# One gathered chunk in every fourth quad replaced by 128 single-row loads from ScalarE's queue

## The chip, the cores and the metric

The kernel runs on one core of a Trainium2 chip. A core has five engines that run their own instruction streams and meet only through semaphores: TensorE (PE, with its weight loads shown apart as PEld), VectorE (DVE), ScalarE (ACT), GpSimd (POOL) and SyncE (SP), and 16 DMA engines that move data between HBM and the on-chip memories. The metric is device time in microseconds (us) of one execution; lower is better. A profiled execution gives a page of summaries and a trace that can be queried.

## The reference

A layer of a graph network with attention: 12,500 nodes with 128 values, 200,000 edges sorted by destination, four heads of 32 values.

```
h = maximum(layernorm(x), 0)
hn = (h @ W_node.T).reshape(N, 4, 32);  e = (edge_attr @ W_edge.T).reshape(E, 4, 32)
att = sum(concat([hn[src], hn[dst], e], -1) * a, -1)
att = where(att > 0, att, 0.2 * att)
m = maximum(segment_max(att, dst), 0);  ex = exp(att - m[dst])
denom = segment_sum(ex, dst) + (E - deg)[:, None] * exp(-m)
out = x + segment_sum((ex / denom[dst])[:, :, None] * hn[src], dst)
```

The costly part for the memory system is `hn[src]`: one row of a node table for each of the 200,000 edges, in random order.

## The kernel before

A first stage computes, for every node, a row of 137 floats (548 bytes) and writes it to a DRAM tensor `table`: the four heads with a one behind each, a count, and the source's part of the attention logit.

Then the edges are worked off in order. A *group* is 511 edges and one slot that carries a running sum from the group before, so 512 slots: four *chunks* of 128. Four groups are a *quad*; there are 392 groups and 98 quads. A super-stage of mostly four quads (the first two and the last six are shorter) shares one softmax pass.

The source rows of a chunk are fetched by one indirect DMA on GpSimd's queue (line 141): 128 row numbers, one in each partition, give 128 rows of `table` in `ga`, a ring of `QUADS = 8` quads. There are 1494 such gathers from `table`, and 72 early ones that read `x` itself while the table is not yet there.

For a quad, `all_logits` (line 817) does the attention logits of its four groups and `sums` (line 745) weighs and sums its four groups, a few quads later. Both are generators, and `together` (line 150) alternates their steps: a step of `sums` for one group, then a step of `all_logits` for one group of a later quad. The order of all instructions is written out by hand in this way (`tc.manual_schedule()`), and each engine executes its own instructions in that order. `all_logits` starts with `flush` (line 829): `add_sources`, line 580 on VectorE, which adds the sources' logits out of `ga` and so needs the whole quad gathered.

A group of sums runs like this. VectorE scales the rows in `ga` by the softmax weights (line 766) and builds a 0/1 matrix `hot` (line 779); TensorE multiplies chunks 1 to 3 (line 784). Then `complete_group` (line 704) of the group before closes the chain that runs through all groups: VectorE forms the carried sum from the last accumulator (line 709), ScalarE copies its count (line 713), TensorE adds chunk 0 (line 714), and ScalarE copies the accumulator out to `pt` (line 715). Line 709 of the next group waits for that copy. At the end of a quad `divide` (line 790) forms the result rows on VectorE, which go out one group at a time.

SyncE issues every other load and store of this stage, in the same order: for each group a window of input rows `xw`, one of results `out` and one of the side table `pw` (line 504); for each quad the edges' features `ea` (line 302) and the destinations `db` (line 307); for each super-stage `dr` (line 532). The row numbers of the windows are loaded into registers by `windows` (line 488, the load itself line 490). ScalarE issues a few loads at the start and four in `checked` (line 861). The transfers of SyncE and ScalarE together take eight semaphores in turn, in the order of the program: a transfer waits, at its issue, until the one eight places before it has landed.

Of the kernel before, what the change touches and what calls it, by code (L numbers as in the profile page):

```python
# [8 lines left out]
F32 = mybir.dt.float32  # L9
BF16 = mybir.dt.bfloat16  # L10
I32 = mybir.dt.int32
AF = mybir.ActivationFunctionType
OP = mybir.AluOpType
AX = mybir.AxisListType

P = 128
# [8 lines left out]
R_CNT, R_SRC, ROW = H * HW, H * HW + 1, H * HW + 5  # L25

J = 4
GE = J * P
NE = GE - 1
WIN = 96  # L30
SPAN = 80
QG = 4
# [4 lines left out]
AT_ONCE = 4  # L37
RAW, MORE = 4, 2
QUADS = 8
SETS = max(NODE_T, QG * J)  # L40
PAD = 1 << 20


def blocks(total, step):
    return [(i, min(step, total - i)) for i in range(0, total, step)]
# [3 lines left out]
def kernel(  # L49
# [35 lines left out]
    nc = tc.nc  # L85
# [8 lines left out]
    table = dram.tile([NP, ROW], F32, name="table")  # L94
# [27 lines left out]
    quads = blocks(G, QG)  # L122
    nq = len(quads)
# [4 lines left out]

    ga_all = consts.tile([P, QUADS, QG, J, ROW], F32, name="ga")
    GA, GATHERED = {}, set()  # L130

    def gather(q, rows, width, lo, hi):

        g0, m = quads[q]
        ga = GA[q] = ga_all[:, q % QUADS]
        for i in range(lo, hi):
            n = -(-min(E - (g0 + i) * NE + 1, GE) // P)
            if n < J:
                nc.vector.memset(ga[:, i, n:, :], 0.0)
            for j in range(n):  # L140
                nc.gpsimd.indirect_dma_start(  # L141
                    out=ga[:, i, j, 0:width], out_offset=None, in_=rows,
                    in_offset=bass.IndirectOffsetOnAxis(ap=srci[:, g0 + i, j:j + 1], axis=0))

    def held_gather(q, i, rows, width):

        nc.vector.memset(ga_all[0:1, q % QUADS, i, 0, 0:1], 0.0)
        gather(q, rows, width, i, i + 1)
# [8 lines left out]
    with tc.manual_schedule():  # L157
# [6 lines left out]
        for _ in range(AT_ONCE):  # L164
            q, i = early.pop(0)
# [12 lines left out]
        with tc.tile_pool(name="prep", bufs=1) as prep, tc.tile_pool(  # L178
            name="prep_ps", bufs=1, space=bass.MemoryType.PSUM
# [21 lines left out]
        def statistics(pool, rows, T):  # L201


            assert nc.vector.BN_STATS_DIM == 6
            stats = pool.tile([P, SETS, 6], F32, name="stats")
            for t in range(T):
# [15 lines left out]
            nc.vector.scalar_tensor_tensor(shift[:, :T], both[:, :T, 0], -0.5, rstd[:, :T],  # L222
# [81 lines left out]
        def fetch_targets(q):  # L304
            g0, m = quads[q]
            db = DB[q] = load.tile([SPAN, QG, GE], I32, name="db", bufs=2)
            nc.sync.dma_start(db[:, :m, :], dst.rearrange("(g e) -> g e", e=GE)[g0:g0 + m]
                              .unsqueeze(0).to_broadcast([SPAN, m, GE]))

        with tc.tile_pool(name="node", bufs=2) as node, tc.tile_pool(  # L310
            name="node_ps", bufs=2, space=bass.MemoryType.PSUM
        ) as node_ps, tc.tile_pool(name="index", bufs=1) as index, tc.tile_pool(
            name="index_ps", bufs=1, space=bass.MemoryType.PSUM
# [112 lines left out]
            for b, (t0, T) in enumerate(sets):  # L426
# [4 lines left out]
                row = node.tile([P, NODE_T, ROW], F32, name="row")  # L431
# [35 lines left out]
    with tc.tile_pool(name="work", bufs=2) as work, \  # L467
# [17 lines left out]

        U8 = mybir.dt.uint8

        def windows(of, size, g, n):

            return nc.values_load_multi_w_load_instructions(  # L490
                of[0:1, g:g + n], engines=[mybir.EngineType.SP], min_val=0, max_val=(N - 1) * size,
                skip_runtime_bounds_check_because="a destination's row, and that is a node")[1]

        as_bytes = lambda d: d.bitcast(U8)
        rows_at = lambda d, at, size: as_bytes(d.rearrange("n c -> (n c)"))[
            bass.ds(at, SPAN * size)].rearrange("(n c) -> n c", c=size)

        due = {"weights": [], "inputs": [], "results": []}

        def issue(*kinds, all_of=False):  # L500

            for kind in kinds:
                for _ in range(len(due[kind]) if all_of else min(1, len(due[kind]))):
                    nc.sync.dma_start(*due[kind].pop(0))
# [16 lines left out]
        def fetch(q):  # L521
            if q not in EA:
                fetch_features(q)
            fetch_windows(q)
            if q not in GATHERED:
                GATHERED.add(q)
                gather(q, table, ROW, raws(q), quads[q][1])

        def fetch_rows(s):
            g0, m = groups(s)  # L530
            dr = DR[s] = turned.tile([SBG * H, NE + 2], I32, name="dr", bufs=2)
            nc.sync.dma_start(dr[0:H * m, :],
                              dst_rows[g0:g0 + m, :].unsqueeze(0).to_broadcast([H, m, NE + 2]))

        def open_logits(q):
            if q == supers[of_quad[q]][0]:
                fetch_rows(of_quad[q])
            if q + 2 < nq:
                fetch(q + 2)
            AT[q] = work.tile([SPAN, QG, GE], BF16, name="at")  # L540
            LG[q] = ps.tile([P, QG, J, PIECES, H], F32, name="lg")

        def logits(q, i):

            g0, m = quads[q]
            if i >= m:
                return
            ea, db, at, lg = EA[q], DB[q], AT[q], LG[q]
            sw = PW[q][:, i, :]
            nc.vector.tensor_tensor(  # L550
                at[:, i, :], node_ps[0:SPAN, g0 + i:g0 + i + 1].to_broadcast([SPAN, GE]),
                db[:, i, :],
                op=OP.is_equal)
            for w in range(2):
                for j in (2 * w, 2 * w + 1):
                    nc.tensor.matmul(lg[:, i, j].rearrange("p k h -> p (k h)"),  # L556
                                     at[:, i, j * P:(j + 1) * P], sw,
                                     start=i + j == 0, stop=False, skip_group_check=True)
                nc.tensor.matmul(lg[:, i, 2 * w:2 * w + 2, 0, :], ea[:, i, w, :], wblk,  # L559
                                 start=False, stop=True, skip_group_check=True)  # L560
# [129 lines left out]

        begun = []
        state = {}

# [8 lines left out]
        def complete_group(q, i, ga, hot, pt, acc, fc):  # L704
            g0, m = quads[q]
            g = g0 + i
            if g:
                before = state["before"]
                nc.vector.tensor_tensor(  # L709
                    ga[0:1, i, 0, 0:H * HW].rearrange("p (h w) -> p h w", w=HW),  # L710
                    before[WIN:WIN + 1, 0:H * HW].rearrange("p (h w) -> p h w", w=HW),
                    fc.unsqueeze(2).to_broadcast([1, H, HW]), op=OP.mult)
                nc.scalar.copy(ga[0:1, i, 0, R_CNT:R_CNT + 1], before[WIN:WIN + 1, R_CNT:R_CNT + 1])  # L713
            nc.tensor.matmul(acc, hot[:, i, 0, :], ga[:, i, 0, :], start=False, stop=True)  # L714
            nc.scalar.copy(pt[:, i, :], acc)  # L715
            state["before"] = acc

            parts = {nq - 1: (2, 3), nq - 2: (2,), nq - 3: (2,)}.get(q, ())
            if i + 1 in parts or i == m - 1:
                lo = max([k for k in parts if k <= i], default=0)  # L720
                den = work.tile([SPAN, QG, H], F32, name="den")
                nc.scalar.activation(den[:, lo:i + 1, :], pt[0:SPAN, lo:i + 1, R_SRC:R_SRC + H],
                                     AF.Exp, scale=-1.0)
                state["division"] = q, pt, den, lo, i + 1
# [92 lines left out]
        def all_logits(q):  # L817
            flush()
            open_logits(q)
            for i in range(QG):  # L820
                logits(q, i)
                issue("weights")
                if i == QG - 1 and q + 2 < nq:
                    issue("weights", all_of=True)
                    fetch_targets(q + 2)
                yield
            state["logits"] = q

        def flush():

            if "logits" in state:
                add_sources(state.pop("logits"))
# [46 lines left out]
        with tc.manual_schedule():  # L879
# [5 lines left out]

            held = [(q, i) for q in range(raw, min(QUADS, nq)) for i in range(raws(q), quads[q][1])]
            GATHERED.update(range(raw, QUADS))

# [247 lines left out]
```

## Time and profile before

| | us |
|---|---|
| median of three runs (2013.32 to 2015.12) | 2014.33 |
| the profiled execution | 2018.52 |
| its span, first to last instruction | 2016.7 |
| GpSimd busy | 1510.6 |
| TensorE busy | 1369.1 |
| VectorE busy | 1323.2 |
| ScalarE busy | 406.3 |

"Busy" counts an engine's own instructions and, for GpSimd, the making of the descriptors for the gathers; instructions by which the other engines issue a DMA are not counted as busy, though the issuing engine cannot go on to its next instruction before they are done. A group line of the page gives the line, the engine, what is written and read, the count, the busy time and the mean of one, and then the engine's idle time just before and what ended it.

### The profile page before, as it was taken

Reading aid. Unit: us, or ns where it says so; the run is one execution under the profiler, and the core shown is the slowest. Engines: PE = TensorE matmul, PEld = TensorE weight load, DVE = VectorE, ACT = ScalarE, POOL = GpSimd, SP = SyncE. Lnnn points to the kernel's source line nnn. Section 1 sums busy time; section 2 is a strip of 40 time slices with the busy share of each in tenths; the row PEclk is TensorE's granted clock in tenths of the full one; section 3 lists DMA queues with packets and bytes.
Section 4 is the critical chain, followed back from the end, with each engine's and each line's share of the span. In section 5 each row is a group of like instructions: output and inputs, shape, how many; then the busy total and the mean of one; then the engine's idle time right before and its main releaser. Section 6 shows DMA issues by size and latency. Waiting matters only on the chain. (4 is left out here: it accounts for less than half of the span.)

```text
span 2016.7 us, 27090 instructions
## 1 busy us (share of the span) xinstructions
PE 1369.1 (68%) x7317; PEld 1243.8 (62%) x7317; DVE 1323.2 (66%) x3261; ACT 406.3 (20%) x1531; POOL 1510.6 (75%) x1609
## 2 busy tenths in 40 slices
PE   6577888766575757666757666666566666777776
PEld 5567788755565746555656566566565565766665
DVE  6676788666574766655656657556566475668776
ACT  6664122111111111111111111111111111112112
POOL 7777777777777777777777777777777777777774
PEclk8777555555555555555555555555555555555556
DMA  7654756544546455455545454545454545454531
GB/s 251 204 145 118 183 162 178 137 129 130 142 122 156 121 146 138 130 131 136 138 130 147 119 146 123 147 120 147 121 145 120 147 122 144 126 146 125 139 96 36
DMA packets 194091, 279.50 MB, mean 139 GB/s; under 512 B 79849, under 2 KB 143337, under 8 KB 186098
## 3 DMA queue, kind: packets, MB, share of 16 engines
q1 hardware_dynamic: 142128, 165.55, 30.0%
q0 software_dynamic: 50112, 109.61, 21.7%
q10 hardware_dynamic: 1698, 2.58, 0.4%
q8 instruction: 61, 1.00, 0.2%
q14 instruction: 92, 0.75, 0.1%
HBM read 254.25 MB, written 23.30 MB: 138 GB/s over the span
## 5 line engine op out<-in xcount | busy, mean ns | idle before, releaser
L141 POOL DMA_INDIRECT ga<-table,srci x1494 | 1422.9, 952 | 457.7 <-issue 384.0
L784 PE MATMUL acc<-ga,hot 128*97 128x137 f32 x2352 | 645.3, 446 | 54.1 <-ACT ga L759 25.4
L784 PEld LDWEIGHTS acc<-ga,hot 128*97 128x97 f32 x2352 | 516.8, 278 | 70.1 <-ACT ga L759 31.4
L556 PEld LDWEIGHTS <-at 80*128 80x128 bf16 x1568 | 211.0, 163 | 521.7 <-DVE at L550 504.4
L556 PE MATMUL lg<-pw,at 80*128 80x12 bf16 x1568 | 169.1, 181 | 445.8 <-DVE at L550 445.1
L559 PE MATMUL lg<-wblk,ea 128*128 128x8 f32 x1568 | 405.0, 356 | 0.0
L559 PEld LDWEIGHTS lg<-wblk,ea 128*128 128x128 f32 x1568 | 377.4, 306 | 0.0
L580 DVE TENSOR_TENSOR U<-st,ga 128x64 f32<-128x64 f32 x98 | 26.2, 268 | 436.1 <-DMA ga<-table,srci 428.8
L550 DVE TENSOR_TENSOR at<-const_ps,db 80x512 bf16<-80x512 f32 x392 | 267.3, 682 | 6.1
L766 DVE TENSOR_TENSOR ga<-ga,ex_ps 128x528 f32<-128x528 f32 x392 | 268.5, 685 | 0.6 <-issue 0.3
L714 PE MATMUL acc<-ga,hot 128*97 128x137 f32 x784 | 257.4, 431 | 2.8 <-ACT ga L713 2.7
L715 ACT COPY pt<-acc 97x137 f32<-97x137 f32 x392 | 107.4, 274 | 717.5 <-PE acc L714 715.1
L714 PEld LDWEIGHTS acc<-ga,hot 128*97 128x97 f32 x784 | 198.3, 282 | 4.9 <-ACT ga L713 4.6
L709 DVE TENSOR_TENSOR ga<-acc,facs 1x132 f32<-1x132 f32 x391 | 115.8, 296 | 121.8 <-ACT pt L715 111.9
L779 DVE TENSOR_TENSOR hot<-const_ps,slot 128x320 f32<-128x320 f32 x384 | 183.5, 478 | 0.0
L713 ACT COPY ga<-acc 1x1 f32<-1x1 f32 x391 | 59.9, 153 | 459.7 <-DVE ga L709 453.1
L141 POOL DMA_INDIRECT ga<-in_x_dram,srci x72 | 68.8, 955 | 23.1 <-issue 18.6
L807 DVE TENSOR_TENSOR res<-pt,const_ps 80x512 f32<-80x512 f32 (+2 forms) x102 | 67.5, 662 | 3.8 <-DVE const_ps L803 0.3
L811 DVE TENSOR_TENSOR res<-res,xw 80x512 f32<-80x512 f32 (+2 forms) x99 | 67.4, 681 | 3.4
L618 ACT ACTIVATE low<-t_ps 64x511 f32<-64x511 f32 (+2 forms) x28 | 16.5, 589 | 190.5 <-PE t_ps L616 190.5
L398 PE MATMUL row_ps<-wcat,hT 128*128 128x137 f32 x198 | 40.8, 358 | 20.7 <-DVE tgt L404 10.7
L568 DVE TENSOR_REDUCE st<-lg 128x64 f32<-128x192 f32 x98 | 35.0, 357 | 25.5 <-PE lg L559 24.6
(137 smaller groups left out, 1012.8 us busy)
## 6 DMA issues: line engine op xcount, KB each, us to landing
db<-in_dst_dram SPq DMA_DIRECT2D x98, 640.0 KB
ea<-in_edge_t_dram SPq DMA_DIRECT2D x98, 512.0 KB
ga<-table,srci POOLq DMA_INDIRECT x1494
xw<-in_x_dram SPq DMA_DIRECT2D x392, 40.0 KB
out_dram<-res SPq DMA_DIRECT2D x392, 40.0 KB
pw<-side SPq DMA_DIRECT2D x392, 1.9 KB
table<-row SPq DMA_DIRECT2D x9, 616.5 KB
xt<-in_x_dram SPq DMA_DIRECT2D x9, 576.0 KB
```

The lines of the kernel that those rows point to most:

```text
L141: nc.gpsimd.indirect_dma_start(out=ga[:, i, j, 0:width], out_offset=None, in_=rows, in_offset=bass.IndirectOffsetOnAxis(ap=srci[:, g0 + i, ...
L550: nc.vector.tensor_tensor(at[:, i, :], node_ps[0:SPAN, g0 + i:g0 + i + 1].to_broadcast([SPAN, GE]), db[:, i, :], op=OP.is_equal)
L556: nc.tensor.matmul(lg[:, i, j].rearrange("p k h -> p (k h)"), at[:, i, j * P:(j + 1) * P], sw, start=i + j == 0, stop=False, skip_group_ch ...
L559: nc.tensor.matmul(lg[:, i, 2 * w:2 * w + 2, 0, :], ea[:, i, w, :], wblk, start=False, stop=True, skip_group_check=True)
L709: nc.vector.tensor_tensor(ga[0:1, i, 0, 0:H * HW].rearrange("p (h w) -> p h w", w=HW), before[WIN:WIN + 1, 0:H * HW].rearrange("p (h w) -> ...
L714: nc.tensor.matmul(acc, hot[:, i, 0, :], ga[:, i, 0, :], start=False, stop=True)
L715: nc.scalar.copy(pt[:, i, :], acc)
L766: nc.vector.tensor_tensor(val, val, weight.unsqueeze(3).to_broadcast([P, J, H, HW]), op=OP.mult)
L779: nc.vector.tensor_tensor(hot[:, i, :, 0:SPAN], lane_ps.unsqueeze(1).to_broadcast([P, J, SPAN]), slot[:, g, :].unsqueeze(2).to_broadcast([ ...
L784: nc.tensor.matmul(acc, hot[:, i, j, :], ga[:, i, j, :], start=j == 1, stop=False)
L807: nc.vector.tensor_tensor(res[:, :n, :].rearrange("p g (h d) -> p g h d", d=HD), val[:, :, :, 0:HD], share_ps[0:R, :n, :].unsqueeze(3).to_ ...
L811: add.tensor_tensor(res[:, :n, :], res[:, :n, :], xw, op=OP.add)
```

## The change

In quads 12, 16, 20, ..., 96 (22 quads) the last chunk of the last group is no longer gathered. Its 128 rows are loaded by 128 DMAs of one row each from ScalarE's queue into a tile `by_row`, which ScalarE copies to its place in `ga` when the logits of that quad begin. Every `complete_group` issues eight of the rows, four after the copy of line 713 and four after the copy of line 715, so that 16 groups load one chunk; the loading runs about four quads ahead of the use. Eight row numbers at a time are loaded into ScalarE's registers. For each such chunk SyncE loads its 128 source numbers (`of`) and VectorE turns them into byte offsets (`at_row`). After 352 groups there is nothing left to load.

```diff
+AHEAD, EVERY, STEP = 12, 4, 4
...
+    whole = lambda g: E - g * NE + 1 >= GE
+    by_row = [q for q in range(AHEAD, nq, EVERY) if quads[q][1] == QG and whole(quads[q][0] + QG - 1)]
+    is_by_row = lambda q, i, j: q in by_row and (i, j) == (QG - 1, J - 1)
...
             for j in range(n):
+                if is_by_row(q, i, j):
+                    continue
                 nc.gpsimd.indirect_dma_start(
...
-        def windows(of, size, g, n):
+        def windows(of, size, g, n, engine=mybir.EngineType.SP):
...
-                of[0:1, g:g + n], engines=[mybir.EngineType.SP], min_val=0, max_val=(N - 1) * size,
+                of[0:1, g:g + n], engines=[engine], min_val=0, max_val=(N - 1) * size,
...
-        rows_at = lambda d, at, size: as_bytes(d.rearrange("n c -> (n c)"))[
-            bass.ds(at, SPAN * size)].rearrange("(n c) -> n c", c=size)
+        rows_at = lambda d, at, size, n=SPAN: as_bytes(d.rearrange("n c -> (n c)"))[
+            bass.ds(at, n * size)].rearrange("(n c) -> n c", c=size)
...
+        def loaded_by_row():
+            def sources_of(q):
+                g = quads[q][0] + QG - 1
+                of = work.tile([1, P], I32, name="of")
+                nc.sync.dma_start(of, src.rearrange("(o e) -> o e", o=1)[:, (g + 1) * GE - P:(g + 1) * GE])
+                return of
+            of = sources_of(by_row[0]) if by_row else None
+            yield
+            for k, q in enumerate(by_row):
+                at_row = work.tile([1, P], I32, name="at_row")
+                nc.vector.tensor_scalar(at_row, of, float(4 * ROW), None, op0=OP.mult)
+                tile_q = work.tile([P, ROW], F32, name="by_row")
+                for p0 in range(0, P, 2 * STEP):
+                    if p0 == P // 2 and k + 1 < len(by_row):
+                        of = sources_of(by_row[k + 1])
+                    at = windows(at_row, 4 * ROW, p0, 2 * STEP, mybir.EngineType.Activation)
+                    for p in range(2 * STEP):
+                        nc.scalar.dma_start(as_bytes(tile_q[p0 + p:p0 + p + 1, :]),
+                                            rows_at(table, at[p], 4 * ROW, 1))
+                        if p0 + p == P - 1:
+                            ROW_TILES[q] = tile_q
+                        if p % STEP == STEP - 1:
+                            yield
...
                 nc.scalar.copy(ga[0:1, i, 0, R_CNT:R_CNT + 1], before[WIN:WIN + 1, R_CNT:R_CNT + 1])
+            next(row_steps, None)
             nc.tensor.matmul(acc, hot[:, i, 0, :], ga[:, i, 0, :], start=False, stop=True)
             nc.scalar.copy(pt[:, i, :], acc)
             state["before"] = acc
+            next(row_steps, None)
...
             open_logits(q)
+            if q in by_row:
+                nc.scalar.copy(GA[q][:, QG - 1, J - 1, :], ROW_TILES.pop(q))
```

More of the change, by code (lines that the diff above doesn't have):

```diff
@@ L486 @@
         U8 = mybir.dt.uint8
-        def windows(of, size, g, n):
+        def windows(of, size, g, n, engine=mybir.EngineType.SP):
             return nc.values_load_multi_w_load_instructions(
-                of[0:1, g:g + n], engines=[mybir.EngineType.SP], min_val=0, max_val=(N - 1) * size,
-                skip_runtime_bounds_check_because="a destination's row, and that is a node")[1]
+                of[0:1, g:g + n], engines=[engine], min_val=0, max_val=(N - 1) * size,
+                skip_runtime_bounds_check_because="a node's row")[1]
         as_bytes = lambda d: d.bitcast(U8)
-        rows_at = lambda d, at, size: as_bytes(d.rearrange("n c -> (n c)"))[
-            bass.ds(at, SPAN * size)].rearrange("(n c) -> n c", c=size)
+        rows_at = lambda d, at, size, n=SPAN: as_bytes(d.rearrange("n c -> (n c)"))[
+            bass.ds(at, n * size)].rearrange("(n c) -> n c", c=size)
         due = {"weights": [], "inputs": [], "results": []}
@@ L689, in softmax @@
             yield
+        ROW_TILES = {}
+        def loaded_by_row():
[21 more added lines that the diff above has]
+                            yield
+        row_steps = loaded_by_row()
+        next(row_steps)
         begun = []
```

## The prediction

> **What bounds the kernel now.** I read the page's share of each engine first, then its costliest groups, the waits, and then stretches of 16 groups.
>
> ```profile
> span 2016.7 us, 27090 instructions
> PE 1369.1 (68%) x7317; PEld 1243.8 (62%) x7317; DVE 1323.2 (66%) x3261; ACT 406.3 (20%) x1531; POOL 1510.6 (75%) x1609
> ...
> L141 POOL DMA_INDIRECT ga<-table,srci x1494 | 1422.9, 952 | 457.7 <-issue 384.0
> ...
> L580 DVE TENSOR_TENSOR U<-st,ga 128x64 f32<-128x64 f32 x98 | 26.2, 268 | 436.1 <-DMA ga<-table,srci 428.8
> ```
>
> 75% looks like slack, but each gather costs GpSimd 0.952 us and about 0.3 us to get to the next one. The waits of GpSimd show that this 0.3 us is no waiting for anybody: 1320 times, never longer.
>
> ```profile
> POOL ga L141 <- issue: 402.6, 1320, 0.3
> POOL ga L141 <- PE acc L784: 31.7, 104, 0.3
> POOL ga L141 <- DMA ga<-table,srci: 24.1, 79, 0.3
> ```
>
> By the trace, the gathers' start times advance 80 to 81 us per 64 gathers from the first (3 us) to the last (1973 us): 1.255 us each, with no gap. GpSimd is the bound from end to end, and VectorE waits 428.8 us for it at line 580. The pace of the others without that bound can be read too. In the columns below (busy and instruction count of PE, PEld, DVE, ACT, POOL, then clock, DMA share, GB/s) each stretch is 16 groups, from one copy at line 715 to the sixteenth after it.
>
> ```profile
> 243.00:300.00 57.00, 51.10 (x272) 47.61 (x272) 47.37 (x110) 11.61 (x50) 43.08 (x46) 0.50 0.61 164
> 300.00:358.00 58.00, 51.58 (x275) 47.92 (x274) 49.04 (x113) 11.63 (x50) 43.90 (x46) 0.50 0.62 164
> 1078.00:1158.00 80.00, 51.25 (x275) 46.89 (x274) 48.79 (x113) 11.63 (x50) 60.65 (x64) 0.52 0.53 134
> ```
>
> Early, with gathers in hand, 16 groups take 57 to 58 us; later, paced by 64 gathers, 80 us. So the consumers have some 22 us of slack per 16 groups.
>
> **What is removed.** 22 of the 1566 gathers. They lie on the path: 22 x 1.255 = 27.6 us, if nothing else becomes the bound: 2018.5 - 27.6 = 1990.9 in the profiled execution's terms. With 63 gathers instead of 64, GpSimd's pace becomes 79 us per 16 groups; the span ends by it if the consumers keep to about 76 (below).
>
> **What is added, on ScalarE.** For 352 groups ScalarE gets eight row loads, one register load, and once per 16 groups a copy of 128x137. Its own queue in the trace:
>
> ```profile
> 541.22 0.27 ACT L715 COPY pt<-acc 97x137 f32<-97x137 f32 x1 [2.13 <-PE acc L714]
> 541.23 0.34 ACTq L861 DMA_DIRECT2D rows<-in_dst_rows_dram  x1
> 541.61 0.22 ACT L737 CAST hot<-is_last 128x16 f32<-128x16 bf16 x1
> ```
>
> Two things are seen here: a DMA issue holds up the next instruction (the cast starts 0.38 us after it), and it runs beside the copy ahead of it (it starts 0.01 us after the copy). So the copies of line 715 disappear behind row loads, and everything else adds up.
>
> *One row load.* A load of one row at an address from a register is not in the trace. The nearest are SyncE's windows at such addresses: 0.34 to 0.37 us, and the next starts 0.45 us after the last (median of 628 pairs; 0.416 the least).
>
> ```profile
> 1418.14 0.34 SPq L504 DMA_DIRECT2D out_dram<-res  x1
> 1418.59 0.36 SPq L504 DMA_DIRECT2D pw<-side  x1
> 1419.05 0.36 SPq L504 DMA_DIRECT2D xw<-in_x_dram  x1
> ```
>
> Fewer rows are a little cheaper: ScalarE's load of eight partitions (line 861, at 703 us) took 0.30 us against 0.33 for 128. I take 0.42: 0.32 and the 0.10 between. Lower end 0.40. The upper end is `ends_i` at line 317, the only load into one partition: 0.71 us, among neighbours at the start that took 0.36 to 0.62; `dr` (line 532) takes 0.63. With the 0.10 that is 0.73 to 0.81; I keep 0.73 as a rival's price, since 0.71 stood right behind a load of 512 pieces. 128 x 0.42 = 53.8 us per 16 groups.
>
> *The register load.*
>
> ```profile
> L490 SPq TENSOR_LOAD <-base_side x98: 295/305/507, 96.3 to 1913.7; - x98
> ```
>
> To the next instruction 0.36 us, at the 90th percentile 0.54; that is for four numbers, here eight. 16 x 0.36 = 5.8 (up to 8.7).
>
> *ScalarE's own work.* 11.63 us per 16 groups (the row above), less 16 copies of line 715 that are now covered (16 x 0.274 = 4.4), more four stretches of semaphore waits ahead of line 759 (0.27 each at 541.64 to 541.92) and the new copy (about 0.3, as line 759): 8.6 us. In a softmax pass it waits for lines 658, 677 and 682: (50.4 + 45.6 + 21.2) / 28 = 4.2 us with nothing to issue in between; its wait for line 616 shrinks when it comes late, that for line 625 is filled by a group of rows.
>
> Sum without waits for transfers: 53.8 + 5.8 + 8.6 + 4.2 = 72.4 us per 16 groups (66 to 81 with the ends above). That is already 14 us over the unpaced 58 and near the 76.
>
> **The waits for landing.** Each of ScalarE's row loads waits until the transfer eight places before it in the order of the program has landed, SyncE's included (the changed order of instructions shows such a wait at every row). Per group 8 rows and 3 to 5 of SyncE's go over eight semaphores, so a row comes about 2.7 us (5.5 x 0.42 and a register load) after its predecessor was issued. Landing times from the trace's records after 450 us: `pw` 2.0 median (2.6 mean), `xw` 2.5 (3.2), `out` 1.9 (2.4), `db` 5.0 (5.2), `ea` 4.9 (5.2). I take 2.0 for a row. Evenly spread, 186 transfers of 2.35 us mean over eight semaphores need 55 us, less than 72. But ScalarE is in order: behind `db` and `ea` it stands about 5.2 - 2.7 = 2.5 us, and `pt`, line 713 and with them the chain of groups stand with it. The two go out 2.5 us apart (1403.92 and 1406.44 us), so I count one stand per quad, 4 x 2.5 = 10 us. From both sides: 0 (all small ones at 2 us and ScalarE late enough for the big ones) and 28 (rows at 3.4 us, the upper quartile of `pw`; then every second predecessor is late).
>
> By the Trainium skill, DMA: Bandwidth & Descriptors, section Anatomy of one DMA, a small transfer costs a fixed time of about 2.0 us, most of it the receipt of the write, whatever its size. The `pw` median agrees; by that rule rows never hold one another and only `db` and `ea` are left. The same page, section Why a DMA increments its semaphore by 16 and not by 1, has a one-partition transfer run on a single DMA engine, the lowest-numbered, so that all rows would queue on one engine; here `ends_i` shows 2 landing marks where a 128-partition load shows 16, which agrees, and it speaks for the upper end.
>
> **Other engines.** The 22 `of` loads on SyncE (0.35 us each) and the 22 `at_row` on VectorE (about 0.3) lie in slack of both: per 16 groups SyncE waits some 27 us for line 811 alone (657.6 us over 98 quads). Without that cover they cost 22 x 0.65 = 14 us. SyncE's own transfers now wait for rows of the same group, but are fetched one or two quads ahead.
>
> **The sum.** 72.4 + 10 = 82.4 us per 16 groups, against GpSimd's 79. ScalarE becomes the bound, and the early stretches at 57 and 58, where the consumers now catch up with GpSimd, are lost as well. The copy of group 16 stands at 243 us before; then 21 stretches of 82.4 = 1730 us to group 352; the last 40 groups, without rows and with gathers in hand, at 57.5 per 16 with the denser softmax passes and the tail, about 150 (163.6 before, paced). 243 + 1730 + 150 = 2123, and 1.8 around the span: 2125 against 2018.5, or 2121 beside the median of 2014.3 (4.2 lower). No change would be at 77.3 per 16 groups ((2016.7 - 393) / 21), GpSimd's full gain at 76.0 ((1989.1 - 393) / 21).
>
> **The rivals.**
> *ScalarE has room, GpSimd stays the bound (faster).* If ScalarE reaches the big transfers' successors late enough and the sum stays at 72.4, it is under 76.0 and the whole gain comes: 1990.9, beside the median 1987. For it: the sum itself, and the even-spread 55 us. Against: a stand of only 1 us per quad uses up the rest. It decides at 0.9 us per quad. 22%.
> *Near the edge:* 77.1 to 77.5 per 16 groups, within 0.2% (about what can be told from no change here): 2014. 4%.
> *Rows land late.* At 3.4 us per row each of five rows in eight stands 0.7 us: 72.4 + 28 = 100 per 16 groups, 243 + 2100 + 150 = 2493. For it: one partition, and the tail of `pw` (4.6 us at the 90th percentile). Against: 2.0 median. 12%.
> *A one-row issue is dear.* 128 x 0.73 = 93.4 in place of 53.8, landings then covered: 112 per 16 groups, 243 + 2352 + 150 = 2745. For it `ends_i` and `dr`, against it the eight-partition load. 10%.
> *The forecast*, 78 to 90 per 16 groups: 2029 to 2281. 52%.
>
> **How the numbers follow.** Faster 22%, same 4%, slower 74%. Time 2121. The range has to take in the faster case and cuts the two dear ones: 1984 to 2340; the forecast's own is 2029 to 2281.
>
> **What would show it.** Right: GpSimd's row with real waits (longer than 0.3 us, for TensorE or ScalarE to free the ring), line 580 no longer waiting for gathers, ScalarE's queue full of issues 0.42 us apart, ScalarE waiting for `db` and `ea`, line 709 waiting for line 715; 16 groups in 82 us before 2050 and below 65 after. Wrong: gathers still 1.255 us apart to the end, the last at about 1945 us, and line 580 still waiting for them.

## The result, and the profile after

| us | before | after |
|---|---|---|
| median | 2014.12 (runs beside it) | 2256.6 (4 runs, 2254.28 to 2269.23) |
| ratio, 95% interval | | 1.1216 (1.1175 to 1.1258) |
| the profiled span | 2016.7 | 2252.4 |
| start of the last gather | 1973 | 2139 |

The changed kernel is 12% slower. The direction and the cause were as forecast, the size was not: 5% had been forecast. Below, a *stand* is the time for which an engine, ready to issue a transfer, waits because the transfer eight places before it has not landed yet. Lines 704, 709, 713, 715 and 580 of before are 741, 746, 750, 753 and 586 in the changed kernel; the row loads are line 720, their register loads line 496, the gathers line 147.

The page after, its shares and the groups that answer to those shown of before:

```profile
span 2252.4 us, 33202 instructions
PE 1418.9 (63%) x7317; PEld 1251.9 (56%) x7317; DVE 1325.5 (59%) x3283; ACT 420.9 (19%) x1553; POOL 1481.8 (66%) x1587
...
L147 POOL DMA_INDIRECT ga<-table,srci x1472 | 1393.9, 947 | 651.5 <-issue 402.0
...
L746 DVE TENSOR_TENSOR ga<-acc,facs 1x132 f32<-1x132 f32 x391 | 115.9, 296 | 634.5 <-ACT pt L753 626.0
...
L753 ACT COPY pt<-acc 97x137 f32<-97x137 f32 x392 | 107.4, 274 | 823.8 <-DMA by_row<-table 607.8
```

ScalarE shows 19% busy and is the bound, since the issuing of DMAs is not counted and waiting for a landing is not either. What gives it away is the idle time ahead of its copies: 823.8 us ahead of line 753. The waits of the changed kernel say the same (total, times, longest):

```profile
DVE ga L746 <- ACT pt L753: 626.0, 252, 5.8
ACT pt L753 <- DMA by_row<-table: 607.8, 281, 4.4
...
POOL ga L147 <- PE acc L752: 222.4, 97, 17.6
```

VectorE's carried sum, a link of the chain of groups, waits 626.0 us for ScalarE's copy. GpSimd, which before never waited longer than 0.3 us for TensorE, now waits up to 17.6 us for the ring to come free. The wait of VectorE for gathers ahead of the sources' logits (428.8 us before) is no longer in the list.

The same stretches of 16 groups as before, in the changed kernel (columns as in the prediction: length, then PE, PEld, DVE, ACT, POOL, clock, DMA share, GB/s):

```profile
153.00:273.00 120.00, 78.37 (x434) 69.46 (x435) 64.29 (x149) 28.57 (x89) 70.92 (x75) 0.56 0.48 117
273.00:359.00 86.00, 52.83 (x266) 46.43 (x265) 47.89 (x111) 12.56 (x52) 58.40 (x63) 0.50 0.49 122
1016.00:1103.00 87.00, 51.98 (x265) 45.48 (x263) 49.05 (x113) 12.04 (x50) 57.83 (x62) 0.50 0.49 122
2101.00:2166.00 65.00, 50.76 (x270) 46.25 (x268) 55.93 (x132) 14.33 (x57) 29.38 (x32) 0.53 0.49 121
```

16 groups take 86 to 87 us from group 16 on, early and late alike, and 65 once no rows are left (group 352, at 2101 us). GpSimd needs 63 x 1.255 = 79 of the 87 us, so it is no longer the bound.

The 129 us between the forecast's span (2123) and 2252.4 are made up as follows: the first 16 groups took 120 us in place of 92, so that group 16 comes at 273 and not at 243 (30); 21 stretches of (2101 - 273) / 21 = 87.05 in place of 82.4 (98); the tail took 151 in place of 150 (1).

**ScalarE's 87 us, term by term.** The rows and their register loads in the trace:

```profile
L720 ACTq DMA_DIRECT2D by_row<-table x2816: 227/234/492, 150.7 to 2099.8; - x188
...
L496 ACTq TENSOR_LOAD <-at_row x352: 709/769/990, 149.8 to 2096.2; - x176
L496 SPq TENSOR_LOAD <-base_side x98: 295/307/578, 97.8 to 2156.5; - x98
```

A row load takes 0.234 us (median), and two follow each other 0.333 us apart when nothing holds them. The register load of eight numbers takes 0.77 us; the queue turns to the first row behind it, by moving its address, 0.84 us after the load began (median), and this first row takes 0.468, 0.234 more than the others. Rows: 128 x 0.333 + 16 x 0.234 = 46.4; register loads: 16 x 0.84 = 13.4.

The stands are read from the records: ahead of each row its address is moved, and what lies between that move and the row above the usual 0.07 us is the stand. There are two kinds, and one place of the changed kernel's queues shows each. First ScalarE's queue, then SyncE's, over the same time:

```profile
1239.72 1.47 ACTq L720 DMA_DIRECT2D by_row<-table  x4
1241.23 0.27 ACT L753 COPY pt<-acc 97x137 f32<-97x137 f32 x1 [2.31 <-DMA by_row<-table]
1243.57 1.23 ACTq L720 DMA_DIRECT2D by_row<-table  x4
1244.84 0.22 ACT L776 CAST hot<-is_last 128x16 f32<-128x16 bf16 x1 [3.34 <-DMA by_row<-table]
```

```profile
1238.76 0.32 SPq L313 DMA_DIRECT2D db<-in_dst_dram  x1
1239.54 0.32 SPq L510 DMA_DIRECT2D xw<-in_x_dram  x1
1239.96 0.41 SPq L510 DMA_DIRECT2D out_dram<-res  x1
1240.72 0.36 SPq L308 DMA_DIRECT2D ea<-in_edge_t_dram  x1
```

The fifth row of the group shares its semaphore with `db`. ScalarE is ready for it at 1241.31, 2.55 us after `db` went out, and it goes at 1243.57, 4.81 after: a stand of 2.26 us, the kind that was forecast at 2.5. The other kind, 10 us earlier:

```profile
1231.37 0.28 ACT L753 COPY pt<-acc 97x137 f32<-97x137 f32 x1 [2.06 <-DMA by_row<-table]
1233.11 1.46 ACTq L720 DMA_DIRECT2D by_row<-table  x3
```

```profile
1231.31 0.34 SPq L510 DMA_DIRECT2D out_dram<-res  x1
1231.76 0.36 SPq L510 DMA_DIRECT2D pw<-side  x1
1232.22 0.36 SPq L510 DMA_DIRECT2D xw<-in_x_dram  x1
```

Here the predecessor of the row at 1233.11 is the store `out` of 1231.31, which lands in 1.8 us. But SyncE issued it only 0.14 us before ScalarE was ready for the row, since it had waited for the result rows from VectorE; so ScalarE stands for nearly all of the landing.

Summed from group 16 to 352, per 16 groups: behind `db` 10.1 (83 stands of 2.56 us), behind `out` 5.2 (68 of 1.59), `pw` 2.3, `xw` 1.6, behind other rows 0.55, behind `ea` 0.4: 20.1 us. Of the 68 stands behind `out`, 61 began less than 1 us after the store was issued (median 0.14), where over all rows with such a predecessor the median is 2.78. So 46.4 + 13.4 + 20.1 = 79.9 of the 87.05 us. The other 7 are a remainder: ScalarE's own work and its waits in the softmax passes, as far as the rows do not cover them.

### The profile page after: what moved, and what is told of

It is laid out like the page before. It is cut to its first block, busy times and chain, and to the rows that moved or that the text cites. A ratio compares the mean times of both kernels' runs of the same rounds, so it can differ in the third digit from the quotient of the medians.

```text
span 2252.4 us, 33202 instructions
## 1 busy us (share of the span) xinstructions
PE 1418.9 (63%) x7317; PEld 1251.9 (56%) x7317; DVE 1325.5 (59%) x3283; ACT 420.9 (19%) x1553; POOL 1481.8 (66%) x1587
## 5 line engine op out<-in xcount | busy, mean ns | idle before, releaser
L147 POOL DMA_INDIRECT ga<-table,srci x1472 | 1393.9, 947 | 651.5 <-issue 402.0
L823 PE MATMUL acc<-ga,hot 128*97 128x137 f32 x2352 | 647.2, 447 | 388.5 <-ACT ga L798 359.7
L823 PEld LDWEIGHTS acc<-ga,hot 128*97 128x97 f32 x2352 | 517.9, 278 | 409.2 <-ACT ga L798 371.3
L746 DVE TENSOR_TENSOR ga<-acc,facs 1x132 f32<-1x132 f32 x391 | 115.9, 296 | 634.5 <-ACT pt L753 626.0
L752 PE MATMUL acc<-ga,hot 128*97 128x137 f32 x784 | 274.8, 453 | 95.8 <-ACT ga L750 95.4
L562 PEld LDWEIGHTS <-at 80*128 80x128 bf16 x1568 | 224.4, 168 | 179.4 <-DVE at L556 156.9
L752 PEld LDWEIGHTS acc<-ga,hot 128*97 128x97 f32 x784 | 180.1, 272 | 153.4 <-ACT ga L750 152.4
L753 ACT COPY pt<-acc 97x137 f32<-97x137 f32 x392 | 107.4, 274 | 823.8 <-DMA by_row<-table 607.8
L678 PE MATMUL ex_ps<-ident,ex 64*128 64x64 f32 (+2 forms) x112 | 18.4, 312 | 126.3 <-ACT ex L665 126.3
L678 PEld LDWEIGHTS ex_ps<-ident,ex 64*128 64x128 f32 (+2 forms) x112 | 13.6, 205 | 129.1 <-ACT ex L665 129.1
L672 DVE SCALAR_TENSOR_TENSOR run<-kp,t_ps 64x511 f32<-64x511 f32 (+2 forms) x28 | 19.0, 678 | 95.6 <-ACT fac L670 95.6
L837 DVE SCALAR_TENSOR_TENSOR den<-pt,den 80x16 f32<-80x16 f32 (+2 forms) x102 | 17.5, 172 | 89.2 <-ACT den L761 88.8
```

Source lines behind the costliest of these rows:

```text
L147: nc.gpsimd.indirect_dma_start(out=ga[:, i, j, 0:width], out_offset=None, in_=rows, in_offset=bass.IndirectOffsetOnAxis(ap=srci[:, g0 + i, ...
L746: nc.vector.tensor_tensor(ga[0:1, i, 0, 0:H * HW].rearrange("p (h w) -> p h w", w=HW), before[WIN:WIN + 1, 0:H * HW].rearrange("p (h w) -> ...
L823: nc.tensor.matmul(acc, hot[:, i, j, :], ga[:, i, j, :], start=j == 1, stop=False)
```

## The experiments

Some runs were on other chips, on which the kernel before itself took 2530 to 2541 us; they stand at the end, apart.

**The removal alone.** The changed kernel without the rows, their register loads and the copy: the 22 chunks are not loaded at all. (The code changes here and below are shown in part; `...` stands for lines that are not shown.)

```diff
-        next(row_steps)
...
-            next(row_steps, None)
...
-            if q in by_row:
-                nc.scalar.copy(GA[q][:, QG - 1, J - 1, :], ROW_TILES.pop(q))
```

> Leaves out the 22 gathers and everything put in their place, so those 22 chunks hold old rows and the output is not the reference's. Theory (GpSimd is the bound of the kernel before, a gather is worth 1.255 us): 2014.1 - 27.6 = 1986.5 us, gathers 1.255 us apart to the end. Rival (the gain is hidden or given back elsewhere, so the change had nothing to win): 2005 or more.

Measured: 1988.92 us beside 2013.15 for the kernel before, ratio 0.9874 (0.9858 to 0.9891), span 1988.1. The bound is the one of before, and the gathers are worth 24.2 us of the 27.6 worked out for them. Its waits:

```profile
POOL ga L147 <- issue: 402.6, 1321, 0.3
DVE U L586 <- DMA ga<-table,srci: 390.7, 64, 10.5
```

So everything above 1989 us in the changed kernel, some 268 us, is the price of the rows.

**The stands, with the issue kept.** From quad 4 on `db` is loaded into one partition and not into 80 (into a tile that stays, so that the logits take old destinations in the other 79).

```diff
+            db = DB[q] = db_all[:, q % 2]
+            n = SPAN if q < 4 else 1
+            nc.sync.dma_start(db[0:n, :m, :], dst.rearrange("(g e) -> g e", e=GE)[g0:g0 + m]
+                              .unsqueeze(0).to_broadcast([n, m, GE]))
```

> The changed kernel, but from quad 4 on the load of the destinations (db) brings one partition instead of 80, so that the comparisons use old destinations in the other 79 and the output is not the reference's. Same number of transfers, same places in the order, a landing near 2 us instead of 5. Theory (ScalarE stands behind db: 83 stands of 2.56 us, 10.1 us per 16 groups): the stands at db go to about 0, 16 groups fall from 87 to 77 to 80, the time to 2256 - 21 x 8 = 2060 to 2120 us. Rival (issue and register loads alone are the bound, the stands hide other waits): 16 groups stay above 85, time above 2220 us.

Measured: 2074.17, ratio 1.0302 (1.0276 to 1.0327). Stands behind `db` fell from 10.1 to 0.07 us per 16 groups, all stands from 20.1 to 12.1, and 16 groups from 87 to 79:

```profile
1016.00:1095.00 79.00, 54.19 (x273) 47.30 (x273) 48.37 (x112) 12.31 (x51) 59.60 (x64) 0.50 0.43 104
```

ScalarE was the bound through the landing of another queue's transfer, and 8 us of stand less is 8 us of time less in each 16 groups. The stands behind `out` and `pw` stayed (5.0 and 3.1). These 79 us are also what GpSimd needs for 63 gathers, and from the 192nd on its gathers do go at 80 to 83 us per 64. But what had been lost before that was not caught up: the kernel ends 108 us after the last gather, where the run without rows ends 46 us after it.

**The issue, with the stands kept.** Rows at addresses fixed in the program in place of addresses from registers, so no register load and no move of an address; other rows of the table are loaded.

```diff
-                    at = windows(at_row, 4 * ROW, p0, 2 * STEP, mybir.EngineType.Activation)
...
+                        nc.scalar.dma_start(tile_q[p0 + p:p0 + p + 1, :],
+                                            table[97 * (p0 + p):97 * (p0 + p) + 1, :])
```

> The changed kernel with row loads at fixed addresses (rows 0, 97, 194, ... of the table) and no register load, so the 22 chunks hold other rows and the output is not the reference's. Theory (issue and register load are ScalarE's largest part): away go 16 x (0.66 until the first row and 0.23 on it) = 14 us and 128 x 0.1 = 13 us of register moves per 16 groups; ScalarE then needs 60 to 70, GpSimd is the bound again, 1985 to 2015 us. Rival (the landing waits alone are the bound): 16 groups stay above 82, time above 2150 us.

Measured: 2039.06, ratio 1.0127 (1.0087 to 1.0167), 77 us per 16 groups. This expectation failed. Gone are the register loads (13.4 us), the slow first rows (3.7) and 0.03 us of each row's spacing (3.7, from 0.333 to 0.305), some 21 us in all, but 16 groups fell by only 10. The stands did not stay as they were seen but moved: behind `db` they grew from 2.56 to 2.83 us each, behind other rows from 0.55 to 3.9 us per 16 groups, 20 in all as before, because ScalarE reaches each row sooner and the landing comes when it comes. Issue time and stands are not independent terms. ScalarE has time to spare again, for its copy of the accumulator now waits for TensorE; the waits here and in the changed kernel:

```profile
ACT pt L752 <- PE acc L751: 530.1, 325, 4.7
```

```profile
ACT pt L753 <- PE acc L752: 165.0, 90, 4.7
```

What paces the groups here, by these waits, is the chain from group to group with the stands in it, and no longer a ScalarE that is never idle. GpSimd's gathers go at 80 to 81 us per 64 from the 192nd on, after one wait of 13.9 us for the ring; the groups behind it gain only 2 us per 16 on it and end 70 us after the last gather.

**Both together.** Fixed rows and the short `db` (the two edits above).

> The kernel of e8_fixed_short a third time, for a chip that runs the kernel before in 2014 us (fixed row addresses without register loads, and db with one partition; output not the reference's). Theory (issue and stand overlap in part, so each alone hid behind the other): 16 groups below 76 us, time 1988 to 2010 us. Rival (a third thing sets 77 to 79): 2030 us or more.

Measured: 1997.39, ratio 0.9919 (0.9899 to 0.9938), 79 us per 16 groups from group 80 on with the gathers 1.26 us apart, as in the run without rows; the total of stands is 6.7. Each alone left the kernel slower than before, both together make it faster: these two costs together are what made the rows dear. The 8 us above the run without rows were lost early: gathers 128 to 192 took 87 us here and 80 there.

**Half the rows.** Eleven chunks (every eighth quad from 16), two rows at a time in place of four, nothing left out.

```diff
-AHEAD, EVERY, STEP = 12, 4, 4
+AHEAD, EVERY, STEP = 16, 8, 2
```

> Every eighth quad from 16 on (11 chunks), two rows after each of the two copies: half the rows for each group, correct output. Theory (ScalarE's issue, register load and stands are the bound at eight rows; at four rows ScalarE needs about half of the 30 us that were added to the unpaced 57.5 per 16 groups, 72 in all, under GpSimd's 79.7): GpSimd stays the bound, 2014.1 - 11 x 1.255 = 2000.3 us. Rival (the loss is proportional to the rows loaded, whatever the pace): 2014 + 242 / 2 = 2135 us.

Measured: 2014.46 (10 runs), ratio 1.0012 (1.0001 to 1.0022): 14 us above what was expected with the full gain of eleven gathers. ScalarE was no longer the bound (4.8 us of stands per 16 groups, 80 us per 64 gathers), yet nothing was gained. The starts of the gathers show a part of why: those from 128 to 192 took 85 us in place of 80, and it is there that GpSimd waited for the ring:

```profile
POOL ga L147 <- issue: 407.7, 1337, 0.3
...
POOL ga L147 <- PE acc L752: 13.6, 28, 5.4
```

In the first 64 groups, where the consumers run at their own 57 to 58 us per 16 groups to catch up with GpSimd, rows take time from them (100 us for the first 16 groups, then 60 to 65), the ring of eight quads comes free late, and what GpSimd loses there never comes back. The trace is of the shortest of the ten executions (2011.3 us), so these 5 us are shown and the rest of the 14 is not.

**Half the rows, late.** Nine chunks (every eighth quad from 32), no row before group 64.

```diff
-AHEAD, EVERY, STEP = 12, 4, 4
+AHEAD, EVERY, STEP = 32, 8, 2
...
-            next(row_steps, None)
+            if g >= 64:
+                next(row_steps, None)
...
-            next(row_steps, None)
+            if g >= 64:
+                next(row_steps, None)
```

> Every eighth quad from 32 on (9 chunks), two rows after each of the two copies, and the loading begins only with group 64, when the consumers have caught up with GpSimd. Correct output. Theory (e3_half lost 4.3 us of its 13.8 in the slow first groups, where rows lengthened the first 64 groups): GpSimd is not held there, 9 x 1.255 = 11.3 us, less some 2 for the tail as in e1_no_rows: 2003 to 2006 us beside a kernel before at 2014. Rival (rows on ScalarE cost time also where GpSimd is the bound): 2010 us or more.

Measured: 2008.71 (10 runs), ratio 0.9975 (0.9965 to 0.9984): faster than both kernels. Beside the kernel before (2013.36) it gains 4.7 us, a quarter of a per cent, where nine gathers are worth 11.3; it is 3 us above the range that was expected. GpSimd loses nothing at the start (80 to 82 us per 64 gathers from the first to the last) and never waits longer than 0.3 us for TensorE:

```profile
POOL ga L147 <- issue: 408.9, 1341, 0.3
...
POOL ga L147 <- PE acc L753: 9.4, 31, 0.3
```

Against the run without rows its tail after the last gather is no worse (46.6 against 45.5). Where the missing 6 to 7 us went stays open. The trace is of the longest of the ten executions (2013.4 us); its gathers take 0.955 us in the mean and those of the run without rows 0.951, which over 1485 gathers makes 6 us in this one execution, but the other nine left no trace.

**The rows on two queues.** All 22 chunks, four rows of each group from ScalarE and four from SyncE.

```diff
-                    at = windows(at_row, 4 * ROW, p0, 2 * STEP, mybir.EngineType.Activation)
+                    at = windows(at_row, 4 * ROW, p0, STEP, mybir.EngineType.Activation)
+                    at += windows(at_row, 4 * ROW, p0 + STEP, STEP)
...
-                        nc.scalar.dma_start(as_bytes(tile_q[p0 + p:p0 + p + 1, :]),
+                        (nc.scalar if p < STEP else nc.sync).dma_start(as_bytes(tile_q[p0 + p:p0 + p + 1, :]),
                                             rows_at(table, at[p], 4 * ROW, 1))
```

> The kernel of h6_shared (22 chunks, four rows of each group from ScalarE, four from SyncE), once more for a chip that runs the kernel before in 2014 us. Theory B (SyncE, in order, stands behind rows, its own loads come late and VectorE waits for xw; on the other chip 9% slower than before where all rows from ScalarE, with the gathers kept, were 4% slower): slower than the changed kernel, 2256 us or more. Theory A (ScalarE is what is short): 1988 to 2003 us.

Measured: 2188.13, ratio 1.0864 (1.0816 to 1.0911), 85 us per 16 groups. Neither forecast of the time held, but the trace shows what theory B describes. ScalarE's stands fell to 1.7 us per 16 groups, for the rows behind `db` and `ea` are now SyncE's, which stands 16.0. But SyncE issues the windows too, and by its waits the bound went to it. They are, in the changed kernel and then in this one:

```profile
SPq L510 <- DVE res L850: 359.9, 93, 12.3
SPq L510 <- DMA by_row<-table: 332.0, 123, 8.2
```

```profile
SPq L721 <- DMA db<-in_dst_dram: 180.3, 64, 4.1
...
SPq L510 <- DVE res L851: 32.9, 6, 12.7
```

SyncE hardly waits for VectorE's results any more (32.9 us); VectorE waits for SyncE's transfers, in this group's line 539.4 us, where it was idle for 3.4 in the changed kernel:

```profile
L851 DVE TENSOR_TENSOR res<-res,xw 80x512 f32<-80x512 f32 (+2 forms) x99 | 67.0, 677 | 539.4 <-DMA out_dram<-res 295.8
```

**On other chips.** Four rows behind the accumulator's copy, none behind the count's, with nine chunks from group 64 on, was meant to tell whether the place of the rows delays the chain. The destinations as four loads of one group each in place of one of a quad, in the changed kernel, was meant to tell whether the size of the transfer ahead decides.

```diff
-AHEAD, EVERY, STEP = 12, 4, 4
+AHEAD, EVERY, STEP = 32, 8, 4
...
-            next(row_steps, None)
             nc.tensor.matmul(acc, hot[:, i, 0, :], ga[:, i, 0, :], start=False, stop=True)
...
-            next(row_steps, None)
+            if g >= 64:
+                next(row_steps, None)
```

> As e10_late_half (9 chunks, from group 64 on, four rows per group, correct output), but all four rows behind the copy of line 715 and none ahead of it, and one register load for two groups. Theory (rows ahead of that copy lengthen the chain that runs through the groups; behind it they lie beside VectorE's carried sum): a little faster than e10_late_half's 2008.7, 2002 to 2006 us. Rival (where the rows stand makes no difference): 2008 to 2010 us.

> Nine chunks by row (quads 32, 40, ..., 96), four rows with each group from group 64 on, all four behind the copy of the accumulator, in place of two behind the count's copy and two behind the accumulator's. Full gain of the nine gathers: 9 x 1.255 = 11.3 us, that is 2002.8 beside 2014.1. With two and two 2008.7 was measured. Theory 'the rows between the count's copy and the accumulator's delay the chain': without them 2002 to 2006. Rival 'only the sum of issue and stands per group counts': 2007 to 2011, as with two and two.

Measured: 2578.39 beside 2530.04, ratio 1.0181 (1.0146 to 1.0215), and again 2575.21 beside 2540.96 for the kernel before, 1.015 (1.012 to 1.0179). Without the version at two and two beside it, this does not tell the two theories apart; whether the place of the rows matters stays open. The trace does tell what is different on these chips: groups 16 to 48, before any row, took 93 us per 16 (57 on the chips of the runs above), and GpSimd, with the same gathers of 0.95 us, waited up to 23.4 us for the ring. By this trace GpSimd is not the bound there, so that little is to be won by taking gathers away from it; that was argued from the trace and not tried.

```diff
+                    if i < quads[q + 2][1]:
+                        nc.sync.dma_start(db_all[:, q % 2, i, :], dst.rearrange("(g e) -> g e", e=GE)[g1:g1 + 1]
+                                          .to_broadcast([SPAN, GE]))
```

> The changed kernel with db loaded in four transfers, one group at a time, each as soon as the same group two quads before has been compared; same bytes, correct output. Theory (the stand at db is its landing time of 5 us less the 2.55 us until ScalarE is there; a quarter of it lands in some 2.5 to 3 us): the stand of 10.1 us per 16 groups goes nearly away, 16 groups near 80 us, the time 2090 to 2150 us. Rival (three more transfers per quad over eight semaphores cost as much): 2220 us or more.

> The changed kernel with the same destinations loaded as four transfers of one group each in place of one of a quad, nothing left out. In the changed kernel the row behind db stands 2.56 us once per quad, 10.1 us per 16 groups, because db lands in about 5 us. Theory 'the size of the transfer ahead decides': a quarter lands in about the time of the other windows (2.0 to 2.6 us), the stands behind db fall from 10 to below 4 us per 16 groups, these take 79 to 83 us in place of 87, and the time is 2080 to 2170. Rival 'every transfer of SyncE between the rows costs a stand': with 12 more transfers per 16 groups the stands stay at 20 us or grow, the pace stays at 87 or more, 2250 or more.

Measured: 2702.97, ratio 1.0661 (1.061 to 1.0711), and again 2680.14, 1.056 (1.0521 to 1.06). A quarter of `db` landed in 2.2 to 2.3 us (a whole one took 4.5 to 4.9 in other versions on these chips), as the first theory has it. But in the second run 226 of 329 rows behind a quarter stand, for 1.30 us each: 14 us per 16 groups, not below 4. Cutting the transfer shortens a stand and multiplies their number.

> All gathers stay, and the row loads are made as well (the copy goes into its own tile instead of into the gathered rows); correct output. Theory (ScalarE sets the pace, the 22 gathers no longer matter): the time of the changed kernel, 2245 to 2265 us. Rival (part of the loss comes from the gathers' ring or their order having changed): clearly below 2245 us, or above 2270 with the 27.6 us of gathers added.

With all gathers kept and the rows loaded beside them into a tile of their own, the ratio was 1.039 (1.0327 to 1.0452). The eleven chunks loaded by SyncE alone:

> Every eighth quad from 16 on (11 chunks), and all four rows of a group go out from SyncE's queue instead of ScalarE's; correct output. Theory (what costs time is that ScalarE, which is in the chain of the groups, issues and stands; SyncE is not in that chain and has the time: 58 transfers x 0.45 + 64 rows x 0.33 + register loads = 57 of 79.7 us per 16 groups): GpSimd stays the bound from the start, without the 4 us that every eighth quad on ScalarE lost in the first 16 groups: 2014.1 - 13.8 = 2000.3 us, 1998 to 2004. Rival (SyncE's loads for the logits come late when it stands behind rows): 2014 us or more.

gave 1.0299 (1.0238 to 1.036). The rows on two queues, three times before the run above:

> The changed kernel (every fourth quad, 22 chunks), but of the eight rows of a group four go out from ScalarE's queue and four, at the same place in the order, from SyncE's; the row eight places after db is then SyncE's. Correct output. Theory: ScalarE has four rows and no stand at db, so it needs under 75 us per 16 groups, SyncE 26 + 21 + 14 = 61; GpSimd is the bound: 1986.5 us and up to 15 for the slow first groups, 1988 to 2003 us. Rival (eight transfers in flight are too few for 11.6 transfers per group, whoever issues them): 16 groups stay above 82 us, time above 2100 us.

> The kernel of e6_shared again (22 chunks, four rows of each group from ScalarE, four from SyncE), since the chip of that call ran the kernel before in 2536 us instead of 2014. Theory (ScalarE is what is short): GpSimd is the bound, 1988 to 2003 us beside a kernel before at 2014. Rival (eight transfers in flight are too few, whoever issues them; e6_shared was 9% slower than the kernel before on its chip): 2150 us or more.

> The kernel of e6_shared a third time, for a chip that runs the kernel before in 2014 us (22 chunks, four rows of each group from ScalarE, four from SyncE). Theory A (ScalarE is what is short): GpSimd is the bound, 1988 to 2003 us. Theory B, after e6_shared and f6_shared lost 9% on the other chip, with VectorE waiting for xw loads (SyncE, in order, stands behind rows and its own transfers come late): 2150 us or more.

gave 1.0918, 1.0921 and 1.0968, about the 1.0864 of the run above. Fixed rows with the short `db`, twice:

> Fixed row addresses without register loads, and db with one partition from quad 4 on, both at once (the 22 chunks hold other rows and 79 of 80 partitions compare with old destinations, so the output is not the reference's). Alone the first took 16 groups from 87 to 77 us and the second to 79. Theory (issue and stand overlap in part, so each alone hid behind the other; without both ScalarE has room): 16 groups at GpSimd's 79 with catching up early below 74, time 1988 to 2010 us. Rival (a third thing sets 77 to 79): 2030 us or more.

> The kernel of e8_fixed_short again (fixed row addresses without register loads, and db with one partition; output not the reference's), for the same reason. Theory (issue and stand overlap in part, so each alone hid behind the other): 16 groups below 76 us, time 1988 to 2010 us. Rival (a third thing sets 77 to 79): 2030 us or more.

gave 1.0107 and 1.0122 (2565.0 and 2566.34), where the run above has 0.9919. So a ratio near 1 does not carry over from the chips above to these, and the runs with all gathers kept and with SyncE alone settle nothing for the others; why the groups take longer on these chips was not found.

## Why the prediction was right, and where it failed

- *The bound and the removal*: right. Without rows the kernel ends at 1989, with GpSimd as the bound.
- *ScalarE becomes the bound, through the chain at lines 709 and 715*: right, by the waits of lines 746 and 753 and the even 86 to 87 us early and late.
- *One row load at 0.42 us*: too dear, 0.333 measured. The rival with 0.73 for one partition was wrong by a factor of two; a load of fewer partitions is cheaper, as the eight-partition load had said. Why `ends_i` took 0.71 the runs don't show.
- *The register load at 0.36*: too cheap, 0.84 to the first row behind it and 0.234 more at that row. The errors cancel by luck: 42.6 + 13.4 + 3.7 = 59.7 us against 53.8 + 5.8 = 59.6.
- *Own work and softmax waits*: 12.8 forecast, 7 left in the accounting. These 6 us too many hid more than half of the next error: the pace was missed by 4.65 us only.
- *The wait for landing, "I count one stand per quad, 4 x 2.5 = 10 us"*: this is the step that failed; the term measured 20.1 us. The stand behind `db` was right in size and number (10.1). What was left out was as much again, 10.0 us, 9.1 of it behind SyncE's windows `out`, `pw` and `xw`. The forecast took each predecessor as issued 2.7 us before its row, by the order of the program. But SyncE's stores go out when VectorE's results are there, and its other windows queue behind those stores, so a predecessor is often issued just as ScalarE gets to the row, and next to nothing of its 2 us of landing is hidden. By the records this is so for `out` and `pw`: 7.1 of their 7.4 us are stands that began less than 1 us after the predecessor was issued. Behind `xw` (1.6 us) it had been issued some 1.55 us before. No experiment moved these issues.
- *The rival that rows land late*: did not come. One-row loads landed in 1.5 us (median; 3.7 at the 90th percentile) and held one another for 0.55 us per 16 groups. By the Trainium skill, DMA: Bandwidth & Descriptors, Anatomy of one DMA, the fixed part of a DMA that GpSimd issues is about 2.0 us; these rows, issued by ScalarE, took a quarter less. What was drawn from that figure, that rows do not hold one another, came true.
- *"The copy of group 16 stands at 243 us before"*: this failed too, for it was taken over unchanged, though rows start with group 0. The first 16 groups, with their denser softmax passes, took 120 us in place of 92: with what group 0 came later, 30 of the 129 us.
- *The tail at 150*: 151.
- *What would show it*: GpSimd's real waits, line 580 without waits for gathers and line 709 waiting came as written, and the pace afterwards was 65 to 66 where below 65 was written.

The faster rival needed less than 0.9 us of stand per quad. With the real stands, 5 us per quad, it was out of reach; with both costs cut most of its gain came (1997, where 1987 had been put).

## What to carry to other kernels

Where two queues take the same few semaphores in turn, as here, a DMA moved to a compute engine costs that engine its issue and also the wait for whatever transfer last took the same semaphore, on either queue. List those predecessors with the time at which each is really issued, not with its place in the program. Issue and stand overlap, so do not take one off alone and expect the time to fall by all of it. Where work is moved off the bound, let it begin only when the consumers have no catching up to do: what the bound lost early at a full ring was not regained here, and the version with fewer rows and a late start was the only one with nothing left out that gained.

## What the runs showed of the hardware

- A load of one row took 0.234 us to issue on ScalarE with an address from a register and 0.263 with a fixed one, against 0.33 for 128 partitions.
- A register load of eight numbers took 0.77 us on ScalarE, one of four 0.31 on SyncE; with the rows on two queues, loads of four took 0.48 on ScalarE and 0.49 on SyncE. The first row behind a load of eight began 0.91 us after the load did and took 0.468, twice the others.
- Of the 2815 one-row loads whose landing is in the records, some 2700 show two landing marks, as `ends_i` did, where windows of 80 partitions mostly show 16. By the Trainium skill, DMA: Bandwidth & Descriptors, Why a DMA increments its semaphore by 16 and not by 1, each DMA engine that takes part adds one at its landing, and the queue adds the rest of the 16 at once; two marks then mean one engine. That the rows queue behind each other there did not show in their stands (0.55 us per 16 groups).
- 16 groups without rows, with gathers in hand, took 57 us on some chips and 93 on others, with the same gathers of 0.95 us; what differs was not found.
